# A gather-bound recommendation kernel: another plan of its last 20 steps, and seven more tiles of rows fetched by SyncE and ScalarE

## The chip, the cores and the metric

The kernel runs on one core of a Trainium2 chip. The metric is device time in microseconds (us), the median of several runs; lower is better.

## What is computed

For each of 16,384 samples the kernel looks up 69 item rows and one label row (96 floats each) in a table of 100,001 rows. Every item row gets an attention weight from a small network over the row and the label; the weighted rows are summed in ten groups (windows of 20, 20, 10, 10, 2, 2, 2, 1, 1, 1 rows), and a "top net" of three layers turns the ten sums and the label into one number. Cut to what matters:

```python
u  = emb[batch_user]                       # 16384 x 69 x 96
q  = emb[batch_label[:, 0]]                # broadcast over the 69 rows
z  = concat([q, u, q - u, q * u])
h  = dice(z @ W1 + b1, a1)                 # 64 wide; dice(x) = (a(1-p) + p) x, p = sigmoid(x)
att = (h @ W2 + b2) @ W3 + b3              # one weight per row
pre = where(batch_user < ITEM_NUM, u * att, 0)
pooled = einsum('gf,bfe->bge', window, pre)
x  = concat([pooled, q])
h  = dice(bn(x @ Wf1 + bf1), af1)          # 200 wide
h  = dice(bn(h @ Wf2 + bf2), af2)          # 80 wide
out = h @ Wf3 + bf3
```

## The kernel before

**Tiles and steps.** The samples come in 32 blocks of 512 (`NBLK`, `BLK`). A block's 64 x 512 main rows and 5 x 512 tail rows are 69 chunks (`NCH`) of 512 rows; a chunk is four tiles of 128 rows. Two chunks are a pair, and one step of the plan handles one pair: 1,104 steps (`NPAIR`). A main chunk holds all 64 main rows of eight samples; a tail chunk holds one tail row of all 512 samples. In the last block the tail chunks stand after the first 20 main chunks (`EARLY`, `chunk_of`). `c` is step 1,096, eight before the end; the steps below are named from it (c-12, c+7), and `d` is what follows the last step.

**Fetching.** Most tiles come by an indirect gather of 128 rows that POOL issues (`gather`, line 266). One tile in some chunks (`SLOT`, the fourth) comes row by row instead: SyncE or ScalarE loads the row offsets into registers, 32 at a time (line 286), and issues 128 small DMAs (line 301) into one of 12 ring buffers, 8 for SyncE, 4 for ScalarE (`Singles`). `SP_CHUNKS` lists SyncE's chunks, 199, one every 5.5 steps, each issued six steps ahead; `ACT_CHUNKS` lists ScalarE's, 170. `scalar_rows(i)` issues 20 of ScalarE's rows in step i, so that its DMAs stand in its queue between the activations; 170 x 128 rows at 20 a step last 1,088 steps, up to c-8.

**A step's work**, as functions that record instructions in program order:

- `fetch_of(i)`: the pair's gathers; eight transposes on PE (`ptr`, line 325), for which PE waits for the rows; four DVE operations (`uT`, the product `quT` with the label; lines 376 and 379). `upool` holds 15 pairs.
- `hidden_of(i)`: the 64-wide layer, eight matmul instructions on PE as the profile counts them (`ph`, lines 399 and 403), two activations on ACT and a product on DVE (`y`, lines 405 to 407). It needs the DVE results of `fetch_of(i)`.
- `rows_of(b, n)`: the attention weights of a band of n pairs: a product with a vector `v2` for each pair (`prow`, line 414) and a copy on ACT (`row`, line 416).
- `spread_of(b, n)`: turns a band's weights by four transposes (`patt`, line 431), and DVE lays them out over the windows (`rw`, line 436).
- `pool_of(i)`: the sums of a pair, 16 matmul instructions with the rows as weights (`acc`, line 325), copied to `pooled` by DVE (line 470). There is one PSUM bank for `acc`. It frees the pair's buffer.
- `tails_of(i)`: the weights of tail chunks (`pa`, `pre`; lines 423 and 424).
- the top net (`top_steps`: eight parts of the first layer, four for each half of its width, then `top2`, `top3`; `dice` on ACT and DVE). Its first-layer sums lie in the one bank of `ps_m`, or for some second halves in `ps_h`. The top net of block 30 runs in steps c-20 to c-16; block 31's is cut into four quarters of 128 samples.

Two engines can't be reordered: each one runs its instructions as the plan records them. The plan is written by hand: `at(step, work...)` appends to a step, and steps are played in order. In the steady part, step i records: the weights of a band of four every fourth step, tails (three behind), the spread of the band one step after its weights, the hidden layer of i-2, ScalarE's rows, the sums of i-7 (`POOL_LAG`), and the fetch of i. From c-8 on the old plan lets the sums and hidden layers catch up by a table of its own (lines 635 to 646): bands of four at c-10, c-6, c-2 are spread a step later, later bands begin at c+2, c+5, c+7; quarters 0 and 1 run at c-7 to c-5 and c-3 to c+1; quarter 2 and quarter 3 run in `d`, behind the last fetch.

Of the kernel before, what the change touches and what calls it, by code (L numbers as in the profile page):

```python
# [18 lines left out]
P = 128  # L19
B, F, E, G = 16384, 69, 96, 10  # L20
# [5 lines left out]
BLK = 512  # L26
NBLK = B // BLK
# [5 lines left out]
NQ = BLK // P  # L33
NT = NCH * 4
NCOL = NT + NQ
NPAIR = NBLK * NCH // 2
# [4 lines left out]
POOL_LAG = 7  # L41
# [3 lines left out]
EARLY = 20  # L45

CLOSE = 8


ROW_BYTES = 4 * E  # L50
SLOT = 3
SP_CHUNKS = [2 * (int(5.5 * s) + 6) + 1 for s in range(199)]
SP_RING = 8
ACT_ROWS = 20
ACT_CHUNKS = [2 * ((s + 1) * P // ACT_ROWS + 2) for s in range(170)]
ACT_RING = 4
SINGLES = SP_CHUNKS + ACT_CHUNKS
NSB = (len(SINGLES) + P - 1) // P
# [4 lines left out]
def chunk_of(c):  # L63

    n, k = divmod(c, NCH)
    if n == NBLK - 1 and k >= EARLY:
        k = NMAIN + k - EARLY if k < EARLY + NTAIL else k - NTAIL
    return n, k
# [47 lines left out]
def rec_kernel(  # L116
# [133 lines left out]
    ps_h = ctx.enter_context(tc.tile_pool(name="ps_h", bufs=2, space=PSUM))  # L250
    ps_x = ctx.enter_context(tc.tile_pool(name="ps_x", bufs=2, space=PSUM))
    ps_acc = ctx.enter_context(tc.tile_pool(name="ps_acc", bufs=1, space=PSUM))
    ps_m = ctx.enter_context(tc.tile_pool(name="ps_m", bufs=1, space=PSUM))
# [226 lines left out]
    def dice(x, g, p, b, weights):  # L480

        sb, sa, sna = weights
        nc.scalar.activation(g, p, AF.Sigmoid, bias=sb, scale=S_BN * S_DICE)
        nc.scalar.activation(g, g, AF.Identity, bias=sa, scale=sna)  # L484
        nc.vector.scalar_tensor_tensor(x, p, b, g, ALU.add, ALU.mult)  # L485
# [3 lines left out]
    def top1(n, cols, h, part, p1):  # L489

        if part == 0:

            banks, tag = (ps_h, "h") if n == NBLK - 1 and cols.start >= BLK // 2 and h == 1 else (ps_m, "m")
            p1 = banks.tile([DH, BLK], F32, tag=tag, name=f"p1_{n}_{h}_{cols.start}")[:, cols]
        for k in range(part * KTOP // 4, (part + 1) * KTOP // 4):
            if k < NTAIL:
                w, x = V[:, k], pres[n][:, k, cols]
            elif k == NTAIL:
                w, x = wf1[:, G], qTs[n % 2][0:E, cols]
            else:  # L500
                w, x = wf1[:, k - NTAIL - 1], pooled[n][:, k - NTAIL - 1, cols]
            nc.tensor.matmul(p1, w[:, h * DH : (h + 1) * DH], x, start=(k == 0), stop=(k == KTOP - 1))  # L502
        if part < 3:
            return p1
        g1 = xpool.tile([DH, BLK], F32, tag="g1", name=f"g1_{n}_{h}_{cols.start}")[:, cols]
        dice(x1s[n][:, h, cols], g1, p1, bf1c[h], dice1[h])

    def top2(n, cols):
        x2 = xpool.tile([D2, BLK], F32, tag="x2", name=f"x2_{n}_{cols.start}")[:, cols]
        g2 = xpool.tile([DH, BLK], F32, tag="g1", name=f"g2_{n}_{cols.start}")[0:D2, cols]  # L510
        p2 = ps_m.tile([D2, BLK], F32, tag="m", name=f"p2_{n}_{cols.start}")[:, cols]
        for i in range(2):
            nc.tensor.matmul(p2, wf2[:, i, :], x1s[n][:, i, cols], start=(i == 0), stop=(i == 1))
        dice(x2, g2, p2, bf2c, dice2)
        return x2
# [8 lines left out]
    def store(n):  # L524

        p4 = ps_x.tile([n, P], F32, tag="x", name="p4")
        nc.tensor.transpose(p4, res[:, 0:n], ident)
        r = ypool.tile([P, 512], F32, tag="y", name="r")[0:n, 0:P]
        nc.vector.tensor_copy(r, p4)
        nc.sync.dma_start(out=out[0 : n * P].rearrange("(m p) o -> m (p o)", p=P), in_=r)  # L530
# [9 lines left out]
    pooled, pres, x1s, x2s, qs, us, hs, ys, bands, rws, p1s = ({} for _ in range(11))  # L540

    def top_steps(n, cols):


        def half(h, part):
            if n not in x1s:
                x1s[n] = xpool.tile([DH, 2, BLK], F32, tag="x1", name=f"x1_{n}")
            p1s[n] = top1(n, cols, h, part, p1s.get(n))

        steps = [lambda h=h, part=part: half(h, part) for h in range(2) for part in range(4)]  # L550
        steps.append(lambda: x2s.__setitem__(n, top2(n, cols)))
        if n * BLK + cols.stop < B:
            steps.append(lambda: top3(n, cols, x2s.pop(n)))
        else:
            steps.append(lambda: top3_last(x2s.pop(n)))
        return steps

    def rows_of(b, n):
        return lambda: attend_rows(b, n)

    def spread_of(b, n):
        return lambda: spread(b, n)

    def pool_of(k):
        return lambda: pool(k)

    def hidden_of(k):
        return lambda: ys.__setitem__(k, hidden(k, *hs[k]))

    def tails_of(k):  # L570
        def work():
            uT = hs.pop(k)[0]
            for j in range(2):
                if chunk_of(2 * k + j)[1] >= NMAIN:
                    attend_tail(k, j, ys[k], uT)

        return work

    def fetch_of(k, between=()):
        def work():  # L580
            for j in range(2):
                n = chunk_of(2 * k + j)[0]
                if n not in pooled:
                    pooled[n] = bpool.tile([E, G, BLK], F32, tag="pooled", name=f"pooled{n}")
                    pres[n] = xpool.tile([E, NTAIL, BLK], F32, tag="pre", name=f"pre{n}")
            u, uT, quT = fetch(k, lambda: [w() for w in between])
            us[k], hs[k] = u, (uT, quT)

        return work
# [4 lines left out]
    def at(step, *work):  # L594
        plan.setdefault(step, []).extend(work)

    by_sync = Singles("sp", nc.sync, mybir.EngineType.SP, SP_CHUNKS, 0, range(SP_RING), 32)
    for s, m in enumerate(SP_CHUNKS):
        at(max(0, m // 2 - 6), lambda s=s: by_sync.fetch(s, 0, P))
# [4 lines left out]
        mybir.EngineType.Activation,  # L604
        ACT_CHUNKS,
        len(SP_CHUNKS),
        range(SP_RING, SP_RING + ACT_RING),
        32,
    )
    def scalar_rows(i):  # L610

        row, stop = i * ACT_ROWS, min((i + 1) * ACT_ROWS, len(ACT_CHUNKS) * P)
        while row < stop:
            s, start = divmod(row, P)
            n = min(P - start, stop - row)
            by_scalar.fetch(s, start, start + n)
            row += n

    c = NPAIR - CLOSE
    for i in range(c):  # L620
        if i >= 3 and (i - 3) % 4 == 3:
            at(i, rows_of(i - 6, 4))
        if i >= 3:
            at(i, tails_of(i - 3))
        if i >= 4 and (i - 4) % 4 == 3:
            at(i, spread_of(i - 7, 4))
        if i >= 2:
            at(i, hidden_of(i - 2))
        at(i, lambda i=i: scalar_rows(i))
        if i < c - CLOSE:  # L630
            if i >= POOL_LAG:
                at(i, pool_of(i - POOL_LAG))
        else:

            for k in {0: (-15, -14), 1: (-13,), 3: (-12, -11), 4: (-10, -9), 7: (-8, -7)}.get(i - c + 8, ()):
                at(i, pool_of(c + k))
        at(i, fetch_of(i))

    at(c, pool_of(c - 6), pool_of(c - 5), tails_of(c - 3), hidden_of(c - 2), fetch_of(c))
    at(c + 1, tails_of(c - 2), hidden_of(c - 1), fetch_of(c + 1))  # L640
    at(c + 2, rows_of(c - 4, 4), tails_of(c - 1), hidden_of(c), spread_of(c - 4, 4), pool_of(c - 4), fetch_of(c + 2))
    at(c + 3, pool_of(c - 3), pool_of(c - 2), hidden_of(c + 1), fetch_of(c + 3, [hidden_of(c + 2)]))
    at(c + 4, pool_of(c - 1), fetch_of(c + 4, [hidden_of(c + 3)]))
    at(c + 5, rows_of(c, 4), spread_of(c, 4), pool_of(c), fetch_of(c + 5, [hidden_of(c + 4)]))
    at(c + 6, pool_of(c + 1), pool_of(c + 2), fetch_of(c + 6, [hidden_of(c + 5)]))
    at(c + 7, pool_of(c + 3), rows_of(c + 4, 2), fetch_of(c + 7, [spread_of(c + 4, 2), hidden_of(c + 6)]))

    for n in range(NBLK):
        first, end = n * NCH // 2, ((n + 1) * NCH - 1) // 2
# [12 lines left out]
    for f in range(NTAIL):  # L662
        at(2 + 2 * f, lambda f=f: tail_weights(f))

    quarter = [top_steps(NBLK - 1, slice(r * P, (r + 1) * P)) for r in range(NQ)]
    for s, step in enumerate([1, 1, 1, 2, 2, 2, 2, 3, 3, 3]):
        at(c - 8 + step, quarter[0][s])
    for s, step in enumerate([5, 5, 5, 5, 6, 6, 6, 6, 7, 9]):
        at(c - 8 + step, quarter[1][s])

    d = NPAIR
    at(d, pool_of(c + 4), hidden_of(c + 7), pool_of(c + 5), *quarter[2][0:4], rows_of(c + 6, 2), quarter[2][4])
    at(d, spread_of(c + 6, 2), *quarter[2][5:8], pool_of(c + 6), quarter[2][8], pool_of(c + 7))
    at(d, quarter[2][9], quarter[3][0], lambda: store(B // P - 1), *quarter[3][1:])

    with tc.manual_schedule():
        qs[0] = head_gather(0)
# [76 lines left out]
```

## Time and profile before

| what | us |
|---|---|
| time, median of 9 runs | 10780.31 (10775.26 to 10786.4) |
| the profiled execution's own time | 10801.49 |
| its span, first to last instruction | 10799.7 |
| PE busy (matmuls) | 8768.3 (81%) |
| POOL busy | 8132.1 (75%) |
| DVE busy | 4240.3 (39%) |
| ACT busy (activations alone) | 1883.9 (17%) |

How to read it: times of one engine's instructions; issuing DMAs on SyncE and ScalarE is not counted as busy, and POOL's gathers are counted with 946 ns each, while one starts every 1,252 ns. PE's share is of an engine whose clock is granted in parts: 0.750 of full speed in the mean over the span. The profile puts each idle stretch of an engine down to what ended it ("<-"); "issue" stands for time in which the engine waited for nothing that the profile shows. The profile's lines show an engine, an operation, "out<-in" by the program's names, and "xcount".

### The profile page before, as it was taken

The numbers are of one execution on the slowest core, as the hardware profiler recorded it, in microseconds if no ns is written. First come the engines' busy times: TensorE is split into PE (matmuls) and PEld (weight loads), VectorE is DVE, ScalarE is ACT, GpSimd is POOL, SyncE is SP. The second block draws the span as 40 slices with busy tenths as digits, with TensorE's granted clock in tenths as the row PEclk, the third lists the DMA queues.
The fourth block names the chain that finished last, engine by engine and source line by source line (L and its number), as shares of the span: only waits on it lengthen the run. The fifth ranks groups of instructions, "written<-read, shape, count | busy, mean of one in ns | idle before, by whom it ended". The sixth has DMA issues, their size and how long they took to land.

```text
span 10799.7 us, 204439 instructions
## 1 busy us (share of the span) xinstructions
PE 8768.3 (81%) x41797; PEld 4312.7 (40%) x41797; DVE 4240.3 (39%) x7535; ACT 1883.9 (17%) x2761; POOL 8132.1 (75%) x8597
## 2 busy tenths in 40 slices
PE   6877888878887888877888788888888787887888
PEld 3334434333443343433343334343444343443335
DVE  4333333333333333333333333333343333333333
ACT  1111111111111111111111111111111111111112
POOL 7777777777777777777777777777777777777776
PEclk6777777777777777777777777777777777777778
DMA  2111111212111111111111111111121111111111
GB/s 50 42 42 42 44 42 42 42 42 44 42 42 42 44 42 42 42 42 45 42 42 42 42 44 42 42 42 42 44 42 42 42 42 44 42 42 42 42 42 35
DMA packets 372495, 460.70 MB, mean 43 GB/s; under 512 B 232114, under 2 KB 232626, under 8 KB 371106
## 3 DMA queue, kind: packets, MB, share of 16 engines
q0 software_dynamic: 274912, 422.81, 16.5%
q1 hardware_dynamic: 52802, 16.36, 1.0%
q10 hardware_dynamic: 43520, 8.44, 0.7%
q14 instruction: 925, 7.58, 0.2%
q8 instruction: 336, 5.51, 0.2%
HBM read 446.81 MB, written 0.07 MB: 41 GB/s over the span
## 4 chain that ended last, share of the span: by engine, by line
POOL 39%; PE 21%; issue 18%; DMA 13%; ACTq 6%; ACT 2%; DVE 1%; another core or an unknown queue 0%; POOLq 0%
POOL u L266 39%; DMA u<-in_rows,ids 13%; ACTq L301 5%; PE acc L325 4%; PE p L502 4%; PE ph L399 3%; PE ph L403 3%; PE ptr L325 3%; ACTq L286 1%; PE prow L414 1%; ACT y L405 1%; POOL q L266 1%; PE ph L396 1%; PE pa L423 1%; PE ph L401 0%
## 5 line engine op out<-in xcount | busy, mean ns | idle before, releaser
L266 POOL DMA_INDIRECT u<-in_rows,ids x8463 | 8009.9, 946 | 2585.1 <-issue 2365.9
L325 PE MATMUL ptr<-ident,u 128*96 128x128 f32 x8463 | 1931.1, 332 | 1623.2 <-DMA u<-in_rows,ids 1572.6
L407 DVE TENSOR_TENSOR y<-ph,y 128x512 f32<-128x512 f32 x1104 | 763.5, 692 | 4950.7 <-ACT y L406 4703.3
L325 PEld LDWEIGHTS acc<-rw,u 128*96 128x96 f32 x15702 | 1678.6, 189 | 1333.2 <-issue 855.9
L325 PEld LDWEIGHTS ptr<-ident,u 128*96 128x96 f32 x8463 | 1132.6, 151 | 2303.3 <-DMA u<-in_rows,ids 1867.6
L325 PE MATMUL acc<-rw,u 128*96 128x20 f32 x15702 | 1796.2, 259 | 201.3 <-DVE rw L436 173.4
L376 DVE COPY uT<-ptr 96x512 f32<-96x512 f32 x2208 | 1489.2, 674 | 770.8 <-PE ptr L325 768.4
L405 ACT ACTIVATE y<-ph 128x512 f32<-128x512 f32 x1104 | 658.9, 597 | 6146.9 <-PE ph L403 3452.2
L399 PE MATMUL ph<-uT,A 128*64 128x512 f32 x4096 | 1599.3, 856 | 0.0
L403 PE MATMUL ph<-quT,wn 96*64 96x512 f32 x4416 | 1549.4, 772 | 0.0
L379 DVE TENSOR_TENSOR quT<-ptr,qT 96x512 f32<-96x512 f32 x2048 | 1379.3, 673 | 0.0
L406 ACT ACTIVATE y<-y,wn,na1c 128x512 f32<-128x512 f32 x1104 | 897.9, 813 | 37.2
L403 PEld LDWEIGHTS ph<-quT,wn 96*64 96x64 f32 x4416 | 429.4, 183 | 1004.0 <-issue 1003.3
L502 PE MATMUL p<-pooled,wf 96*100 96x512 f32 (+1 forms) x1400 | 646.3, 607 | 0.0
L414 PE MATMUL prow<-y,v 128*32 128x512 f32 x2208 | 514.5, 878 | 70.2 <-DVE y L407 64.4
L399 PEld LDWEIGHTS ph<-uT,A 128*64 128x64 f32 x4096 | 259.5, 172 | 608.6 <-issue 604.0
L416 ACT COPY row<-prow 128x512 f32<-128x512 f32 (+1 forms) x277 | 161.8, 584 | 1733.2 <-issue 549.9
L470 DVE COPY pooled<-acc 96x160 f32<-96x160 f32 x1008 | 420.5, 417 | 110.4 <-PE acc L325 107.9
L502 PE MATMUL p<-pre,V 96*100 96x512 f32 (+1 forms) x700 | 394.0, 708 | 9.6 <-DVE x L485 9.2
L502 PEld LDWEIGHTS p<-pooled,wf 96*100 96x100 f32 x1400 | 243.5, 186 | 303.9 <-issue 303.9
L436 DVE SCALAR_TENSOR_TENSOR rw<-patt,bb,wn 128x320 f32<-128x320 f32 x554 | 276.0, 538 | 124.6 <-PE patt L431 123.8
L485 DVE SCALAR_TENSOR_TENSOR x<-p,wf,g 100x512 f32<-100x512 f32 (+3 forms) x105 | 73.9, 704 | 516.5 <-ACT g L484 516.5
(72 smaller groups left out, 2716.9 us busy)
## 6 DMA issues: line engine op xcount, KB each, us to landing
ring<-in_rows SPq DMA_DIRECT2D x25472, 0.4 KB
ring<-in_rows ACTq DMA_DIRECT2D x21760, 0.4 KB
u<-in_rows,ids POOLq DMA_INDIRECT x8463
ids<-in_idx SPq DMA_DIRECT2D x8, 560.0 KB, 3.9
q<-in_emb,ids POOLq DMA_INDIRECT x128
wf<-in_far SPq DMA_DIRECT2D x1, 1209.0 KB, 8.8
wn<-in_near SPq DMA_DIRECT2D x1, 236.0 KB, 3.1
offsets<-in_single_rows SPq DMA_DIRECT2D x1, 192.0 KB, 2.5
```

Of the source, the lines that this page charges most:

```text
L266: nc.gpsimd.indirect_dma_start(out=dst, out_offset=None, in_=table, in_offset=bass.IndirectOffsetOnAxis(ap=index, axis=0),)
L301: d = self.engine.dma_start(out=ring[r : r + 1, b], in_=row_bytes[:, bass.ds(self.values[r], ROW_BYTES)]).then_inc(self.sems[k], 16)
L325: ins = op(out, ring[:, at[0]].bitcast(F32) if at else u[:, 4 * (c % 2) + t, :], other, **how)
L376: nc.vector.tensor_copy(uT[j][0:E], ptr)
L379: nc.vector.tensor_tensor(quT[:, j, :].rearrange("e (s f) -> e s f", f=FM), ptr.rearrange("e (s f) -> e s f", f=FM), by_field(q[:, k * NS ...
L399: nc.tensor.matmul(p, As[n % 2][:, k // 4, :], uT[j], start=True, stop=False)
L403: nc.tensor.matmul(p, Wp, quT[:, j, :], start=False, stop=True)
L405: nc.scalar.activation(y, ph, AF.Sigmoid, scale=S_DICE)
L406: nc.scalar.activation(y, y, AF.Identity, bias=a1c, scale=na1c)
L407: nc.vector.tensor_mul(y, ph, y)
L414: nc.tensor.matmul(pr[32 * k : 32 * (k + 1), :], v2, ys[b + k], start=True, stop=True)
L502: nc.tensor.matmul(p1, w[:, h * DH : (h + 1) * DH], x, start=(k == 0), stop=(k == KTOP - 1))
```

## The change

- SyncE's tiles: one every 5.33 steps, 205 instead of 199. ScalarE's tiles: 171 instead of 170, and `scalar_rows` is recorded up to the last steps, so its 128 more rows are issued in steps c-8 to c-2.
- The plan from step c-12 on is written anew. Hidden layers run one step behind their fetch. In odd steps from c-9 on (counted from c) a band of two pairs, i-3 and i-2, is weighted and spread in one step, around the hidden layer of i-1; in even steps the sums of i-4 and i-3 are made. The steps c-12 to c-7 lead over from the old lag of seven.
- The quarters of block 31's top net stand in a table, `QUARTERS`: quarter 0 in c-12 to c-7, quarter 1 in c-5 to c, quarter 2 in c+3 to c+7 with its last part in `d`; quarter 3 remains in `d`, with the first parts of both its halves ahead of the last band.
- Only quarter 3's second half has its sums in `ps_h`; the sums in progress are kept for each half, since the two halves of quarter 3 now overlap.

```diff
+QUARTERS = [
+    [-12, -12, -11, -11, -10, -10, -9, -9, -8, -7],
+    [-5, -5, -5, -4, -3, -3, -3, -2, -1, 0],
+    [3, 3, 3, 4, 5, 5, 5, 6, 7],
+]
-SP_CHUNKS = [2 * (int(5.5 * s) + 6) + 1 for s in range(199)]
+SP_CHUNKS = [2 * (int(5.33 * s) + 6) + 1 for s in range(205)]
-ACT_CHUNKS = [2 * ((s + 1) * P // ACT_ROWS + 2) for s in range(170)]
+ACT_CHUNKS = [2 * ((s + 1) * P // ACT_ROWS + 2) for s in range(171)]
...
-            banks, tag = (ps_h, "h") if n == NBLK - 1 and cols.start >= BLK // 2 and h == 1 else (ps_m, "m")
+            banks, tag = (ps_h, "h") if n == NBLK - 1 and cols.start == BLK - P and h == 1 else (ps_m, "m")
...
-            p1s[n] = top1(n, cols, h, part, p1s.get(n))
+            p1s[n, h] = top1(n, cols, h, part, p1s.get((n, h)))
...
     c = NPAIR - CLOSE
-    for i in range(c):
+    for i in range(c - 12):
...
-        if i < c - CLOSE:
-            if i >= POOL_LAG:
-                at(i, pool_of(i - POOL_LAG))
-        else:
-
-            for k in {0: (-15, -14), 1: (-13,), 3: (-12, -11), 4: (-10, -9), 7: (-8, -7)}.get(i - c + 8, ()):
-                at(i, pool_of(c + k))
+        if i >= POOL_LAG:
+            at(i, pool_of(i - POOL_LAG))
         at(i, fetch_of(i))
 
-    at(c, pool_of(c - 6), pool_of(c - 5), tails_of(c - 3), hidden_of(c - 2), fetch_of(c))
...
-    at(c + 7, pool_of(c + 3), rows_of(c + 4, 2), fetch_of(c + 7, [spread_of(c + 4, 2), hidden_of(c + 6)]))
+    quarter = [top_steps(NBLK - 1, slice(r * P, (r + 1) * P)) for r in range(NQ)]
+
+    for i in range(c - 12, NPAIR):
+        band = i - 3 if (i - c) % 2 and i > c - 11 else None
+        if i == c - 12:
+            at(i, pool_of(c - 19), tails_of(c - 15), hidden_of(c - 14))
+        elif i == c - 11:
+            at(i, pool_of(c - 18), tails_of(c - 14), rows_of(c - 16, 4))
+        elif i == c - 10:
+            at(i, pool_of(c - 17), pool_of(c - 16), pool_of(c - 15))
+        elif i == c - 9:
+            at(i, pool_of(c - 14))
+        elif i == c - 8:
+            at(i, pool_of(c - 13), pool_of(c - 12))
+        elif i == c - 7:
+            at(i, pool_of(c - 11))
+        elif band is None:
+            at(i, pool_of(i - 4), pool_of(i - 3))
+        if band is not None:
+            at(i, rows_of(band, 2))
+        if i > c - 12:
+            at(i, tails_of(i - 2))
+        at(i, hidden_of(i - 1), lambda i=i: scalar_rows(i))
+        if i == c - 11:
+            at(i, spread_of(c - 16, 4))
+        if band is not None:
+            at(i, spread_of(band, 2))
+        for r, steps in enumerate(QUARTERS):
+            at(i, *[work for step, work in zip(steps, quarter[r]) if c + step == i])
+        at(i, fetch_of(i))
...
-    d = NPAIR
-    at(d, pool_of(c + 4), hidden_of(c + 7), pool_of(c + 5), *quarter[2][0:4], rows_of(c + 6, 2), quarter[2][4])
-    at(d, spread_of(c + 6, 2), *quarter[2][5:8], pool_of(c + 6), quarter[2][8], pool_of(c + 7))
-    at(d, quarter[2][9], quarter[3][0], lambda: store(B // P - 1), *quarter[3][1:])
+    d, last = NPAIR, quarter[3]
+    at(d, pool_of(c + 4), hidden_of(c + 7), pool_of(c + 5), quarter[2][9], last[0], rows_of(c + 6, 2))
+    at(d, last[4], lambda: store(B // P - 1), spread_of(c + 6, 2), pool_of(c + 6), pool_of(c + 7))
+    at(d, *last[1:4], *last[5:])
```

More of the change, by code (lines that the diff above doesn't have):

```diff
@@ L629, in rec_kernel @@
         at(i, lambda i=i: scalar_rows(i))
-        if i < c - CLOSE:
-            if i >= POOL_LAG:
-                at(i, pool_of(i - POOL_LAG))
-        else:
-            for k in {0: (-15, -14), 1: (-13,), 3: (-12, -11), 4: (-10, -9), 7: (-8, -7)}.get(i - c + 8, ()):
-                at(i, pool_of(c + k))
-        at(i, fetch_of(i))
-    at(c, pool_of(c - 6), pool_of(c - 5), tails_of(c - 3), hidden_of(c - 2), fetch_of(c))
-    at(c + 1, tails_of(c - 2), hidden_of(c - 1), fetch_of(c + 1))
-    at(c + 2, rows_of(c - 4, 4), tails_of(c - 1), hidden_of(c), spread_of(c - 4, 4), pool_of(c - 4), fetch_of(c + 2))
@@ L642, in rec_kernel @@
[L642 to L645, printed above, removed]
-    at(c + 7, pool_of(c + 3), rows_of(c + 4, 2), fetch_of(c + 7, [spread_of(c + 4, 2), hidden_of(c + 6)]))
+        if i >= POOL_LAG:
+            at(i, pool_of(i - POOL_LAG))
@@ L663, in rec_kernel @@
         at(2 + 2 * f, lambda f=f: tail_weights(f))
[L665 to L669, printed above, removed]
-    d = NPAIR
-    at(d, pool_of(c + 4), hidden_of(c + 7), pool_of(c + 5), *quarter[2][0:4], rows_of(c + 6, 2), quarter[2][4])
-    at(d, spread_of(c + 6, 2), *quarter[2][5:8], pool_of(c + 6), quarter[2][8], pool_of(c + 7))
-    at(d, quarter[2][9], quarter[3][0], lambda: store(B // P - 1), *quarter[3][1:])
+    d, last = NPAIR, quarter[3]
+    at(d, pool_of(c + 4), hidden_of(c + 7), pool_of(c + 5), quarter[2][9], last[0], rows_of(c + 6, 2))
+    at(d, last[4], lambda: store(B // P - 1), spread_of(c + 6, 2), pool_of(c + 6), pool_of(c + 7))
+    at(d, *last[1:4], *last[5:])
     with tc.manual_schedule():
```

## The prediction

> **What bounds the kernel now.** I read the page's table of groups first, then who waited for whom on POOL, then the chain of waits, then the last 300 us as a table by stage, and last the timeline there. On the page and among POOL's waits:
>
> ```profile
> POOL 39%; PE 21%; issue 18%; DMA 13%; ACTq 6%; ACT 2%; DVE 1%; another core or an unknown queue 0%; POOLq 0%
> L266 POOL DMA_INDIRECT u<-in_rows,ids x8463 | 8009.9, 946 | 2585.1 <-issue 2365.9
> POOL u L266 <- issue: 2365.9, 7745, 0.3
> ```
>
> POOL never waits longer than 0.3 us before a gather: 8,591 gathers (128 of them for the labels) run back to back from 3.2 to 10758.6 us, one each 1.252 us, or 9.74 us for one of the 1,104 steps. Up to the last stretch each gather costs its full 1.252 us. The end looks different:
>
> ```profile
> 10498.57 0.45 PE L325 MATMUL ptr<-ident,u 128*96 128x128 f32 x1 [0.85 <-DMA u<-in_rows,ids]
> ...
> 10757.67 0.96 POOL L266 DMA_INDIRECT u<-in_rows,ids  x1 [0.30 <-issue]
> ...
> 10765.26 0.64 PE L325 MATMUL ptr<-ident,u 128*96 128x128 f32 x4
> ...
> 10797.47 0.24 SPq L538 DMA_DIRECT2D out<-r  x1
> ```
>
> The first line is the last time that PE waits for a gather, at step c-20 (c is step 1096). From there the chain of waits holds PE and short ACT and DVE links only. PE's waits from 10498 us to the end, and the stages:
>
> ```profile
> PE acc L325 <- DVE pooled L470: 9.8, 8, 2.7
> PE p L521 <- DVE x L485: 9.2, 2, 7.8
> PE prow L414 <- DVE y L407: 4.7, 2, 4.0
> ...
> PE ptr L325 <- DMA u<-in_rows,ids: 0.8, 1, 0.8
> ```
>
> ```profile
> 10400.00:10498.00 98.00, 76.61 (x330) 35.49 (x329) 41.84 (x73) 15.18 (x22) 74.19 (x79) 0.71 0.17 41
> 10498.00:10591.00 93.00, 82.41 (x369) 39.49 (x370) 32.74 (x57) 15.43 (x22) 70.37 (x75) 0.85 0.17 41
> 10591.00:10766.00 175.00, 146.11 (x847) 91.64 (x847) 75.88 (x139) 37.47 (x59) 126.80 (x134) 0.80 0.16 39
> 10766.00:10800.00 34.00, 28.20 (x220) 23.40 (x218) 7.54 (x19) 7.96 (x17) 0.00 (x0) 0.89 0.01 3
> ```
>
> The first figure after each length is PE's busy time, the 0.71 to 0.89 the granted clock. So 10,500 us are POOL's, and the last 300 us are PE's own: its work, plus 28.9 us of waits from 10591 to 10766 and 5.8 us behind. PE runs some 20 us late at step c-13 and 5 us late at the last step (the last gather starts at 10757.67, its rows reach PE at 10765.26). ACT matters for one reason:
>
> ```profile
> 10594.86 8.64 ACTq L301 DMA_DIRECT2D ring<-in_rows  x20
> 10603.55 0.60 ACT L405 ACTIVATE y<-ph 128x512 f32<-128x512 f32 x1 [7.94 <-issue]
> 10605.77 1.92 PE L414 MATMUL prow<-y,v 128*32 128x512 f32 x2 [4.03 <-DVE y L407]
> ```
>
> ACT issues 20 rows a step in 5.99 us, 8.6 to 8.9 us where a load of 32 addresses falls between them; an activation behind them waits, and here PE with it.
>
> **The change, part by part.** *Gathers.* 376 tiles by row replace 369: seven gathers fewer, 8.8 us by POOL's pace. By step c-20 six are gone (201 SyncE tiles are due by then against 195), so PE leaves its last gather wait 6 x 1.252 = 7.5 us sooner. What comes after is PE's, so I count 7.5; 8.8 is the other end.
>
> *Can SyncE deliver?* The timeline has 503 of its rows in 199.68 us, 0.397 us each, 50.8 us a tile. Tiles are due every 5.33 steps, 51.9 us by the steps' 9.73 us. The first tile's rows are out at 55.7 us and due when step 6 ends, at 78 us; rounding to whole steps eats at most one step of 9.7 us. The lead of some 20 us thus stays positive and grows. I count nothing; if it failed, PE would wait for rows, and POOL's 15 buffers would still let it run on. The 171st ScalarE tile is dearer: rows are issued 20 a step, so 128 more occupy ACT for 6.4 more steps, c-8 to c-2, where it was free before.
>
> *Work moved.* The sums come 3 to 4 steps behind instead of 7, hidden layers one step behind, the last block's quarters earlier. All of it stays inside the stretch that PE bounds, so moved matmuls cost what they cost before: zero. What is seen as a shorter end is paid ahead of it: behind the last transposes stood 31.8 us up to the last store's issue (10765.9 to 10797.5); without quarter 2 (3.56 and 3.84 us of matmuls, and its waits) it is about 23.9, but those 7.9 us are now in steps c+3 to c+7.
>
> *Work added.* Ten bands of two and one of four replace five of four and two of two: four more bands, each one product with v (1.00 us at full clock for two y as for four, 1.74 at half) and four transposes (0.44, 0.80): 5.8 to 10.2 us. I take 5.8, since a slower matmul leaves less of the waits beside it.
>
> *Waits.* In an odd step the new order is: product of the two newest y, hidden layer, transposes of that band, all in one step, where a whole fetch lay between band and transposes before. I lay two steps out from the end of a hidden layer, by the rows (full / half clock): fetch 1.01 / 1.87, hidden 1.90 / 3.61, sum 1.30 / 2.69; y 1.45 on ACT and 0.69 on DVE; copies 2.7 for a pair on DVE. While ACT issues rows, it is free 0.7 + 7.6 us after the hidden layer (7.6 = 5.99 + 0.62 x 2.6), then copies the band in 0.6: PE's transposes start at 8.9, the next sum after y and weights at 11.8, the second sum after DVE's copies at 14.9, the next hidden layer ends at 18.1 (full) or 21.2 (half). PE's work in it is 10.0 or 19.0. At the granted 0.80 (six tenths full) that is 5.7 us of waits in two steps, 4 where parts of the top net fill some. Without rows on ACT the same layout gives 14.6 and 19.9, so 3.1, or 2 with parts. Four pairs of steps of the first kind (c-10 to c-2): 19; four of the second: 10. Beside them the end, with nearly the same last chain of 4 us: 5.8. Together 35, against 28.9 + 5.8 = 34.7: zero. Ends: if ACT's rows cost no wait, its four pairs have 3.1 us in place of 5.7, -10; with a load in every step (8.7 instead of 7.6 us, 2 us a pair) and one dice waiting 7.8 as above, +16. Queued behind PE's wait are the next fetch's transposes, then DVE's copies; POOL does not wait, 15 buffers against a lag of 3 to 4 steps.
>
> The Trainium skill, TensorE: Matmul & The Clock Gate, section "A second HAM failure mode: psum-queue depth-cycling", speaks against the change: a PE that idles briefly between groups of matmuls lets its clock gate swing back to half rate, and bands of two make more such groups. The trace agrees in direction only: 0.71 where PE waits for gathers, 0.85 in the backlog, though single waits there are short. By that rule I would take the steady 0.75 in place of 0.80: 146 x (0.80 / 0.75 - 1) = +10 us in the sum. I leave it out.
>
> *Sum.* -7.5 + 0 + 5.8 + 0 = -1.7 us. The profiled execution took 10801.5 us (span 10799.7, 1.8 around it); -1.7 gives 10799.8. It stands 21.2 us over the median of 10780.3, a difference I leave alone: 10778.6, rounded to 10778.
>
> **Rivals.** *PE catches up.* If PE's waits shrink far enough that it stands beside the last gather again (0.6 us late, as at c-20, not 5), the whole 8.8 us count, and the shorter end too: the last rows land some 1.2 us after the gather's end, 10758.6 + 1.2 - 8.8 = 10751.0, + 0.6 + 0.6 for the transposes, + 23.9, + 2.2 for the store = 10778.3 against 10799.7: -21.4, 10759. For it: PE's work in two steps is 10.0 us at full clock against 19.5 of gathers, which is enough to make up 20 us. Against it: ACT's rows until c-2, and quarters in between. No plan of the end can gain much more.
>
> *ACT's queue decides (slower).* Place: the transposes of bands in c-11, c-9, c-7, c-5, c-3. If PE reaches each while ACT has just begun its rows, each waits a whole issue, 5 x 8.6 = 43 in place of the 19 counted, and one dice behind rows holds the only bank of the top net's sums for 7.8: -1.7 + 24 + 7.8 = +30, 10810. It decides once those waits are over some 43 us together. For it: the 4.03 us above. Against: products and hidden layer lie ahead of the transposes and cover 4 to 6 us.
>
> *The rows come late.* SyncE delivers slower than 51.9 us a tile and PE, not POOL, is held by it: the gain of 7.5 is lost, 10786. Against: 0.397 us a row over hundreds of rows.
>
> **How the numbers follow.** Forecast 0.71, PE catches up 0.16, ACT's queue 0.11, late rows 0.02. 0.2% is 21.6 us, about what a measurement of this kernel can tell from no change. Faster by more: half of the catching up and the forecast's edge, 0.10. Slower by more: ACT's queue and an edge, 0.12. Within: 0.78. The forecast's own range is -12 to +19 by the ends of the waits and bands, 10768 to 10799; from 10758 (PE caught up) to 10799 about 2 in 10 are left out, most of them above.
>
> **What would show it.** POOL: 8,584 gathers in all, the last ending near 10750, still no wait over 0.3 us. PE: last wait for a gather near 10491, last transposes near 10770, not 10765, the end some 24 us behind its last four transposes. Waits of PE from c-12 on: 30 to 40 us, with the transposes of bands (L436 in the new file) waiting for the copy of ACT among the largest; before they had 0.7 us. A clock below 0.78 from c-12 on, or PE waiting for gathers in the last five steps, would prove the sum wrong; so would a POOL wait.

## The result and the profile after

The changed kernel takes 10813.59 us (median of 10 runs, 10809.96 to 10817.09) where the kernel before takes 10780.86 (30 runs): 1.0030 of it [1.0022, 1.0038], or 32.7 us more. Beside each other on another chip, later, the two took 10815.03 and 10782.28: again 32.8. The forecast was 10778, its range ended at 10799.

The two profiled executions stand closer, 10816.73 and 10801.49, because the one of before had slower gathers. From the first gather to the last, one took 1.2520 us there and 1.2494 after; over 8,590 gathers that is 22 us, about the 21 us by which the profile of before stood over its median. So stages are compared from step c-20 on, not from the span's start.

The page of after (the chain of waits by engine; the costliest group) and POOL's waits (total, times, longest):

```profile
POOL 41%; PE 20%; issue 18%; DMA 13%; ACTq 5%; ACT 1%; DVE 1%; another core or an unknown queue 0%; POOLq 0%; DVEq 0%
L271 POOL DMA_INDIRECT u<-in_rows,ids x8456 | 7982.6, 944 | 2581.5 <-issue 2358.9
POOL u L271 <- issue: 2358.9, 7727, 0.3
```

POOL is as before: 8,584 gathers, no wait over 0.3 us. (Line numbers are five higher: 325 is now 330, 399 is 404, 416 is 421.) The end, from the timeline of after:

```profile
10469.42 0.45 PE L330 MATMUL ptr<-ident,u 128*96 128x128 f32 x1 [0.82 <-DMA u<-in_rows,ids]
...
10726.43 0.95 POOL L271 DMA_INDIRECT u<-in_rows,ids  x1 [0.30 <-issue]
...
10780.84 1.04 PE L330 MATMUL ptr<-ident,u 128*96 128x128 f32 x8
...
10812.70 0.24 SPq L543 DMA_DIRECT2D out<-r  x1
```

PE's last wait for a gather is at c-20, as before. But the last transposes stand 54 us behind the start of the last gather, where before 7.6 us lay between them. PE falls further and further back up to step c (61 us, in a table below) and makes up little of it. The windows of after, cut at the end of the last transposes of c-20, c-13, c-10, c and c+7 (length, then busy time with instructions of PE, PE's weight loads, DVE, ACT and POOL, then the granted clock):

```profile
10469.90:10563.00 93.10, 84.24 (x340) 39.83 (x339) 31.20 (x55) 16.83 (x24) 70.19 (x76) 0.78 0.18 42
10563.00:10597.00 34.00, 27.42 (x163) 17.91 (x162) 13.90 (x26) 6.88 (x11) 25.77 (x28) 0.85 0.17 41
10597.00:10720.00 123.00, 93.30 (x486) 59.18 (x484) 39.84 (x78) 20.76 (x35) 93.00 (x99) 0.72 0.17 41
10720.00:10782.00 62.00, 56.65 (x310) 32.97 (x308) 26.45 (x51) 14.22 (x24) 5.67 (x6) 0.81 0.03 6
10782.00:10815.00 33.00, 25.23 (x153) 18.88 (x153) 8.09 (x21) 4.89 (x10) 0.00 (x0) 0.75 0.01 3
```

The same cut made in other kernels' traces; in each field length / PE's idle time / granted clock. 205/170 stands for 205 tiles by SyncE and 170 by ScalarE. The last three columns are kernels of the experiments below; "new plan 205/168" is new_plan_205_168_d.

| stage | before | after | old plan 205/170 | new plan 205/170 | new plan 205/168 |
|---|---|---|---|---|---|
| c-20 to c-13 | 87.8 / 10.0 / 0.85 | 93.2 / 8.9 / 0.78 | 87.8 / 10.2 / 0.85 | 88.1 / 10.4 / 0.85 | 81.7 / 4.6 / 0.88 |
| c-13 to c-10 | 26.2 / 6.8 / 0.80 | 34.1 / 6.6 / 0.85 | 26.2 / 6.2 / 0.74 | 34.6 / 6.1 / 0.85 | 26.5 / 0.6 / 0.87 |
| c-10 to c | 93.7 / 15.2 / 0.80 | 123.1 / 29.7 / 0.72 | 93.7 / 15.2 / 0.80 | 99.0 / 13.7 / 0.79 | 91.5 / 9.6 / 0.81 |
| c to c+7 | 59.1 / 7.0 / 0.80 | 61.7 / 5.2 / 0.81 | 59.0 / 7.0 / 0.80 | 60.0 / 5.3 / 0.86 | 63.8 / 7.5 / 0.86 |
| behind c+7 | 33.8 / 5.5 / 0.89 | 33.1 / 7.8 / 0.75 | 33.8 / 5.5 / 0.89 | 31.6 / 7.8 / 0.80 | 32.8 / 7.1 / 0.71 |
| sum | 300.7 / 44.5 | 345.1 / 58.2 | 300.5 / 44.1 | 313.3 / 43.3 | 296.3 / 29.4 |

After against before: 44.4 us more from c-20 on, while six gathers fewer, 7.5 us by count, lie ahead of it. Of the 44.4 us, 13.7 are idle time; in the other 30.7 PE is busy, with nearly the same work (1,445 matmul records against 1,430), at a mean clock of 0.77 against 0.82. The largest piece is c-10 to c, 29 us. What PE waits for from c-20 on, in after:

```profile
PE ph L404 <- DVE uT L381: 16.9, 3, 8.3
PE acc L330 <- DVE pooled L475: 13.2, 10, 3.4
PE patt L436 <- ACT row L421: 8.8, 3, 4.0
PE p L526 <- DVE x L490: 8.0, 1, 8.0
```

The first line is new: before, from c-20 on, no matmul of a hidden layer waited for `uT`. One of the three, with all that ACT, DVE and PE did around it (start, duration):

```profile
10669.63 8.88 ACTq L306 DMA_DIRECT2D ring<-in_rows  x20
10678.61 0.37 ACT L488 ACTIVATE g<-p,dice 100x128 f32<-100x128 f32 x1 [8.23 <-issue]
10679.01 0.49 ACT L489 ACTIVATE g<-g,dice,dice 100x128 f32<-100x128 f32 x1
10679.42 0.56 ACT L421 COPY row<-prow 64x512 f32<-64x512 f32 x1
...
10679.54 0.35 DVE L490 SCALAR_TENSOR_TENSOR x<-p,wf,g 100x128 f32<-100x128 f32 x1 [8.44 <-ACT g L489]
10679.81 0.68 DVE L381 COPY uT<-ptr 96x512 f32<-96x512 f32 x1
...
10666.95 1.08 PE L404 MATMUL ph<-uT,A 128*64 128x512 f32 x4
...
10669.78 1.04 PE L330 MATMUL ptr<-ident,u 128*96 128x128 f32 x8
10670.75 1.46 PE L419 MATMUL prow<-y,v 128*32 128x512 f32 x4
10680.54 2.31 PE L404 MATMUL ph<-uT,A 128*64 128x512 f32 x3 [8.33 <-DVE uT L381]
```

Read it from top to bottom. ACT issues the step's 20 rows for 8.88 us. The dice activation recorded behind them waits for all of it, though the top net's matmuls that it reads had ended at 10669.94, 0.3 us after the rows began. DVE's half of the dice stands at the head of DVE's own queue and waits with it (8.44 us). Behind it in that queue stand the copies of rows that PE transposed at 10669.78. The next hidden layer needs them, so PE stands for 8.33 us. After that three matmuls take 2.31 us where four took 1.08 us ahead of the wait. A part of it is a wait for the pair's second `uT` copy (10681.00), but the clock has fallen too, from 0.92 ahead of the wait to 0.50 behind it:

```profile
10660.00:10670.00 10.00, 8.82 (x71) 7.31 (x70) 3.24 (x6) 1.03 (x2) 7.56 (x8) 0.92 0.17 40
10680.50:10685.40 4.90, 4.86 (x9) 1.33 (x9) 1.78 (x3) 0.00 (x0) 3.68 (x5) 0.50 0.19 44
```

### The profile page after: what moved, and what is told of

Read it like the earlier page. It is cut to its first block, busy times and chain, and to the rows that moved or that the text cites. A ratio compares the mean times of both kernels' runs of the same rounds, so it can differ in the third digit from the quotient of the medians.

```text
span 10814.9 us, 206305 instructions
## 1 busy us (share of the span) xinstructions
PE 8761.0 (81%) x41813; PEld 4309.5 (40%) x41813; DVE 4243.2 (39%) x7543; ACT 1885.6 (17%) x2765; POOL 8104.5 (75%) x8590
## 4 chain that ended last, share of the span: by engine, by line
POOL 41%; PE 20%; issue 18%; DMA 13%; ACTq 5%; ACT 1%; DVE 1%; another core or an unknown queue 0%; POOLq 0%; DVEq 0%
POOL u L271 40%; DMA u<-in_rows,ids 13%; ACTq L306 4%; PE p L507 4%; PE acc L330 4%; PE ph L404 3%; PE ph L408 3%; PE ptr L330 2%; PE prow L419 1%; ACTq L291 1%; POOL q L271 1%; ACT y L410 1%; PE ph L401 0%; PE pa L428 0%; PE ph L406 0%
## 5 line engine op out<-in xcount | busy, mean ns | idle before, releaser
L404 PE MATMUL ph<-uT,A 128*64 128x512 f32 x4096 | 1602.9, 855 | 17.2 <-DVE uT L381 16.9
L441 DVE SCALAR_TENSOR_TENSOR rw<-patt,bb,wn 128x320 f32<-128x320 f32 (+1 forms) x562 | 277.3, 534 | 111.8 <-PE patt L436 108.3
```

The source lines that it names most:

```text
L404: nc.tensor.matmul(p, As[n % 2][:, k // 4, :], uT[j], start=True, stop=False)
```

## The experiments

**1. The change taken apart.** Two things change: the number of tiles and the plan. Four kernels mix them. Theory Q lays the loss on activations queued behind ScalarE's rows, theory W on the new order of work itself; theories L and F, further down, each lay it on one piece of that order. Each is the kernel before or after with one or two lines of the other:

```diff
 old_plan_205_170 (against before)
-SP_CHUNKS = [2 * (int(5.5 * s) + 6) + 1 for s in range(199)]
+SP_CHUNKS = [2 * (int(5.33 * s) + 6) + 1 for s in range(205)]
 old_plan_205_171: that, and
-ACT_CHUNKS = [2 * ((s + 1) * P // ACT_ROWS + 2) for s in range(170)]
+ACT_CHUNKS = [2 * ((s + 1) * P // ACT_ROWS + 2) for s in range(171)]
 new_plan_199_170: after, with both lists as before
 new_plan_205_170: after, with ACT_CHUNKS as before
```

> The old plan of the end with six more SyncE tiles (205), ScalarE's left at 170. Both theories: six gathers less, all of them ahead of the stretch that PE bounds: 6 x 1.25 = 7.5 us off, 10773 against 10781. If SyncE could not deliver 205 tiles, no gain or a loss, with PE waiting for rows.

> The old plan with 205 and 171 tiles: ScalarE's rows last 6.4 steps longer, to c-2. Theory Q (ScalarE's queue: activations behind rows are late, DVE's operation on them heads DVE's queue, PE waits for the copies behind it): the dice of quarters 0 and 1 now stand behind rows, so it loses: 10785 to 10800. Theory W (it is the new order of work, bands of two and a lower clock, that costs): 8 us off as with 170, 10772.

> The new plan with the old tiles: rows end at c-8. Theory Q: most of the loss goes with the rows of c-8 to c-2, though seven gathers come back: 10795 to 10802. Theory W: the loss stays and the gathers come back: 10820.

> The changed kernel without its 171st ScalarE tile. Theory Q: PE's waits for DVE's copies at c-7 and c-3 (6.3 and 8.3 us) and for bands at c-5 and c-3 go: 15 to 25 us off 10814, 10789 to 10798. Theory W: 10812, unchanged but for one gather.

| kernel (one chip) | us | against before |
|---|---|---|
| before | 10786.68 | |
| old plan, 205/170 | 10777.48 | -9.2, 0.9992 [0.9982, 1.0001] |
| old plan, 205/171 | 10797.87 | +11.2, 1.0010 [1.0001, 1.0020] |
| new plan, 199/170 | 10805.14 | +18.5, 1.0015 [1.0006, 1.0025] |
| new plan, 205/170 | 10793.13 | +6.5, 1.0005 [0.9996, 1.0015] |

Both parts lose. By their distance to before, theory Q put the last three rows at +4 to +19, +14 to +21 and +8 to +17, theory W at -9, +39 and +31: Q holds for two and misses the third by little, W is far off. The six SyncE tiles are worth 9.2 us in the old plan (an interval of -19 to +1, which doesn't exclude zero), 12.0 in the new. The 171st ScalarE tile costs 20.4 us in the old plan, though it saves a gather; in the new plan it costs some 26 (32.7 - 6.5, from two chips). The plan alone, at 205/170, costs 15.6.

The table of stages shows where that lies: from c-20 on PE idles 44.1 us in the old plan and 43.3 in the new, but is busy for 256.4 us in the one and 270.0 in the other, at nearly the same mean clock (0.82 and 0.83). Most of it is the hidden layers, first of old_plan_205_170, then of new_plan_205_170 (number of matmuls, busy time of the line, mean ns of one):

```profile
L403 PE MATMUL ph<-quT,wn 96*64 96x512 f32 x116 | 38.8, 698 | 0.0
L399 PE MATMUL ph<-uT,A 128*64 128x512 f32 x106 | 38.8, 768 | 0.0
```

```profile
L408 PE MATMUL ph<-quT,wn 96*64 96x512 f32 x116 | 48.9, 741 | 0.0
L404 PE MATMUL ph<-uT,A 128*64 128x512 f32 x106 | 47.2, 770 | 2.4 <-DVE uT L381 1.8
```

As many matmuls, of nearly the same mean length, take longer: they lie less over one another. The new plan records a hidden layer one step behind its fetch, ahead of the next fetch, and its weight loads wait 17.2 us for `uT` in 19 short waits, against 1.3 us in 2 in the old plan.

In the old plan the 171st tile costs in another way than in the new one. PE's waits of old_plan_205_171 from c-20 on, and the longest in its timeline:

```profile
PE p L502 <- DVE x L485: 11.2, 1, 11.2
...
PE p L513 <- DVE x L485: 6.0, 2, 4.9
```

```profile
10619.94 8.88 ACTq L301 DMA_DIRECT2D ring<-in_rows  x20
...
10630.05 6.08 ACTq L301 DMA_DIRECT2D ring<-in_rows  x20
10636.17 0.37 ACT L483 ACTIVATE g<-p,dice 100x128 f32<-100x128 f32 x1 [5.38 <-issue]
```

There the parts of a quarter are recorded close together, and the next half of the top net waits for its bank until the dice has read it, 11.2 us. It is the same late activation, with another victim.

**2. The rows behind the dice.** In the changed kernel, `scalar_rows` is recorded behind the parts of the top net:

```diff
-        at(i, hidden_of(i - 1), lambda i=i: scalar_rows(i))
+        at(i, hidden_of(i - 1))
...
-        at(i, fetch_of(i))
+        at(i, lambda i=i: scalar_rows(i), fetch_of(i))
```

> The same kernel as rows_behind_parts, whose first run fell on a chip where SyncE issued a row in 0.666 us instead of 0.397, so that every kernel took 16.7 ms or more and GpSimd and TensorE waited for rows: it says nothing of the last 300 us. Where SyncE delivers, theory Q: 10790 to 10798 beside 10781 of the kernel before (the changed kernel took 10814), TensorE's waits for uT 3 us or less and the clock from c-10 to c 0.78 or more. Rival (the 171st tile costs wherever its rows stand): 10808 to 10818, the waits at the bands or the y instead.

10814.69 us beside 10793.59 of before on its chip: +21.1 us, 1.0018 [1.0009, 1.0027], where the changed kernel stands at +32.8 on another chip. So 11.7 us come back, about half of what was expected. The waits for `uT` are gone from PE's list, and c-10 to c falls from 123.1 to 109.9 us with the clock back at 0.80; but the activations now late are the bands' copies. PE's waits from c-20 on, then two lines of ACT:

```profile
PE patt L436 <- ACT row L421: 19.3, 5, 5.0
PE acc L330 <- DVE pooled L475: 10.6, 10, 1.7
```

```profile
10602.40 8.86 ACTq L306 DMA_DIRECT2D ring<-in_rows  x20
10611.30 0.58 ACT L421 COPY row<-prow 64x512 f32<-64x512 f32 x1 [8.16 <-issue]
```

By the 10780.86 of before that would be 10802, between the two expectations. The queue theory gets about half of what it expected by way of the dice; waits for the next activation took the place of the others, as the rival had said. In both places tried, something that PE needs soon stands behind the 6 to 9 us of row issues.

**3. No rows in the last 20 steps.** ScalarE gets 168 tiles, so that its last rows are issued at c-21; everything else is the new, or the old plan with 205 SyncE tiles.

```diff
-ACT_CHUNKS = [2 * ((s + 1) * P // ACT_ROWS + 2) for s in range(171)]
+ACT_CHUNKS = [2 * ((s + 1) * P // ACT_ROWS + 2) for s in range(168)]
```

> The same kernel as old_plan_205_168, for the same reason. Theory Q (rows behind which activations stand cost, gathers in TensorE's stretch don't): 10770 to 10776 where the kernel before takes 10781 to 10787. Rival (GpSimd's pace still counts to the end): 10778 to 10784.

> The same kernel as new_plan_205_168, for the same reason. Theory Q alone (the plan's loss at 205/170, 15.6 us, is its activations behind rows in c-12 to c-8, but for four more bands): within 8 us above the old plan with 205 and 168 tiles. Theory W (the loss lies in the order of work, which leaves short waits of weight loads and of sums that no longer lie beside other work): 10 to 18 us above it, with the stages c-13 to c-10 and c-10 to c as long as in the new plan with 205 and 170 tiles (34.6 and 99.0 us) or within 3 us of that.

On one chip, before at 10793.59: the old plan takes 10784.16 (-9.4, 0.9990 [0.9981, 0.9999]), the new plan 10780.16 (-13.4, 0.9987 [0.9978, 0.9996]). So without rows the new plan isn't 10 to 18 us behind the old one, as theory W had it, but 4 us ahead (the traces say 2.7: 298.7 against 296.0 us from c-20 on), and the queue theory had expected a small loss for the four bands. The old plan fell short of that theory too: it was to gain some 11 us, and gains no more than with 170 tiles (-9.2). Both plans lose idle time without the rows, the old one 11.7 us, the new one 13.9, and PE remains busy in the new plan for 267 us. What evens them out is the clock of the old plan, 0.67 from c-10 to c where it was 0.80 with 170 tiles:

```profile
10579.20:10688.10 108.90, 93.42 (x489) 63.66 (x487) 40.90 (x75) 20.43 (x34) 82.25 (x87) 0.67 0.20 40
```

What this fall hangs on is not shown; no wait of PE from c-20 on was over 2.6 us there. Two extra gathers cost nothing that shows in the old plan; in the new one PE's last transposes stand beside the last gather (below), so there they may cost. Then the pair that matters, on one chip:

> The new plan with 205 and 168 tiles beside the changed kernel on one chip where SyncE delivers. Theory Q: 40 to 50 us below the changed kernel and 8 to 18 us below the kernel before. Rival (the 46 us came of comparing two chips): less than 35 us below the changed kernel.

> The changed kernel on the same chip: 28 to 38 us above the kernel before; the partner of the new plan with 168 ScalarE tiles.

Before 10782.28, new plan 205/168 10769.27 (-13.0, 0.9988 [0.9979, 0.9997]), the changed kernel 10815.03 (+32.8, 1.0030 [1.0019, 1.0042]): 45.8 us between the last two, for three ScalarE tiles. This is the version that beats both. Its PE waits from c-20 on, and the last transposes:

```profile
PE acc L330 <- DVE pooled L475: 11.0, 9, 1.9
PE ptr L330 <- DMA u<-in_rows,ids: 3.6, 5, 1.1
...
PE ph L404 <- DVE uT L381: 0.5, 1, 0.5
```

```profile
10732.58 0.45 PE L330 MATMUL ptr<-ident,u 128*96 128x128 f32 x1 [0.97 <-DMA u<-in_rows,ids]
```

PE waits for gathers again, up to the very last one. How far PE's last transpose of a step lags behind its landed rows, in us, by the traces:

| kernel | c-20 | c-13 | c-10 | c-4 | c | c+4 | c+7 |
|---|---|---|---|---|---|---|---|
| before | 0.4 | 22 | 19 | 23 | 17 | 8 | 6 |
| old plan 205/168 | 0.4 | 17 | 1.2 | 14 | 12 | 4 | 1.7 |
| new plan 205/170 | 1.1 | 24 | 29 | 32 | 32 | 28 | 22 |
| after | 0.6 | 29 | 33 | 49 | 61 | 57 | 53 |
| new plan 205/168 | 0.4 | 16 | 13 | 8 | 7 | 1.4 | 0.4 |

The old plan bunches the quarters: without rows its PE has caught up by c-10 and then falls back at quarters 0 and 1. The new plan spreads them, which pays only if PE isn't held up meanwhile.

**4. One moved part.** In the old plan with 205/170, quarter 2 goes ahead of the last transposes; in the new plan with 205/168, it goes back behind them. The choice of the bank goes with it both times, and in the new plan the first parts of quarter 3 go back behind the last band, so the two moves aren't quite each other's reverse.

```diff
 old_plan_205_170_q2 (against old_plan_205_170; the ps_h bank as in the change)
-    at(c + 5, rows_of(c, 4), spread_of(c, 4), pool_of(c), fetch_of(c + 5, [hidden_of(c + 4)]))
+    at(c + 5, rows_of(c, 4), spread_of(c, 4), pool_of(c), *quarter[2][0:4], fetch_of(c + 5, [hidden_of(c + 4)]))
...
 (parts 4 to 6 in c + 6, parts 7 and 8 in c + 7, the last in d)
 new_plan_205_168_q2end (against new_plan_205_168)
-    [3, 3, 3, 4, 5, 5, 5, 6, 7],
...
 (d as in the kernel before)
```

> The old plan with 205 and 170 tiles (10777.5 beside 10786.7) and one part of the change: the third quarter of the last block's top net is recorded in steps c+5 to c+7 instead of behind the last transposes. The prediction's reading (moved work costs what it cost before): 0, within 3 us of the old plan with 205 and 170 tiles; the end behind the last transposes falls from 33.8 by 7.9 to about 26 us, and the stage c to c+7 grows by as much. Theory F (the quarter filled waits for y, bands and weights at the end, and fills none where it goes): the end falls by 2 to 4 us only, c to c+7 grows by 6 to 8, and the kernel is 3 to 6 us slower.

> The same kernel as new_plan_205_168_q2end, whose first run fell on a chip that issues SyncE's rows slowly (the kernel before took 16734 us there). Theory F: 4 to 9 us below the new plan with 205 and 168 tiles on the same chip. Rival (TensorE has caught up by c+7, the quarter hides in waits for gathers): 0 to 4 us above it, with a longer end behind the last transposes.

Old plan: 10793.06 beside 10793.59 of before, -0.5, where its partner stands at -9.2: the move costs 8.7 us (by way of before, on two chips, each good to some 10 us; the two traces say 6.8 from c-20 on, 307.3 against 300.5). New plan: 10775.97 with the quarter at the end, 10769.27 with it moved, on one chip, with ranges that don't overlap: the move gains 6.7 us. The windows c to c+7 and behind, first of old_plan_205_170, then of old_plan_205_170_q2:

```profile
10683.60:10742.60 59.00, 52.01 (x286) 30.03 (x285) 29.16 (x53) 12.10 (x18) 38.72 (x41) 0.80 0.18 36
10742.60:10776.40 33.80, 28.32 (x222) 23.53 (x220) 7.54 (x19) 8.09 (x17) 0.00 (x0) 0.89 0.01 3
```

```profile
10692.10:10761.70 69.60, 61.33 (x353) 41.22 (x354) 30.00 (x56) 14.75 (x24) 37.82 (x40) 0.80 0.15 30
10761.70:10791.30 29.60, 22.78 (x152) 17.84 (x151) 6.50 (x16) 5.44 (x11) 0.00 (x0) 0.83 0.01 3
```

The quarter adds 10.6 us where it goes and takes 4.2 from where it was: without it, PE idles 6.8 us at the end instead of 5.5, at a clock of 0.83 instead of 0.89. In the new plan the same two stages are 62.3 and 37.1 us with the quarter at the end, 63.8 and 32.8 with it moved; PE idles 10.4 us in c to c+7 in the first, 7.5 in the second, in part for gathers. There a part of the quarter's work lies in time that PE would have waited anyway. Theory F is right for the old plan, its rival for the new, in direction: both moves were worth more than either had said.

**5. Two chips with a slower SyncE.** Seven runs, among them the first ones of experiments 2 to 4, fell on two chips where the kernel before took 16772.24 and 16734.09 us. All had 205 SyncE tiles, and all were slower than before by 1.0115 to 1.0150, the changed kernel by 1.0150 [1.0133, 1.0167]. Their times tell nothing of the end. SyncE's rows in a stretch of 200 us, in old_plan_205_170, then in old_plan_205_168 and its chain of waits:

```profile
5000.62 199.52 SPq L301 DMA_DIRECT2D ring<-in_rows  x502
```

```profile
5000.57 198.97 SPq L301 DMA_DIRECT2D ring<-in_rows  x299
```

```profile
SPq 63%; issue 36%; PE 1%; another core or an unknown queue 0%; DMA 0%; ACT 0%; DVE 0%; ACTq 0%
```

One row takes 0.397 us to issue on the first chip, 0.665 on the second: there SyncE bounds the whole kernel, and kernels with six more tiles on it are 199 to 246 us slower. Why it is slower there is not known. One kernel ran on such a chip only: the new plan with 205/168 whose hidden layer and bands are recorded inside the next fetch.

> As new_plan_205_168, but the hidden layer of step i-1 and the transposes of a band are recorded within the fetch of step i, behind the transposes of its first chunk, as the old plan did from c+3 on; everything else of the new plan stays. Theory L: the weight loads' waits for uT fall below 4 us in all, and the time lies 8 to 15 us below new_plan_205_168, within 6 us of the old plan with 205 and 168 tiles. Theory W (bands of two, 16 more transposes and the new order of work cost the rest, by the clock or by matmuls that no longer overlap): within 5 us of new_plan_205_168.

Its weight loads waited 3.7 us for `uT` instead of 43.4 in its partner on that chip, but `prow` then waited 16.9 us in 9 times for `y`. Its time, 17009.9 beside 16986.97, is set by SyncE and settles nothing. Its trace does show that the place of the hidden layers makes their matmuls spread out: the lines of `ph` are busy for 44.5 and 41.7 us there, 53.0 and 55.9 in its partner. What that is worth where SyncE delivers was not measured. Theory L's sum fell in another way: in new_plan_205_168_b weight loads still wait 13.6 us for `uT`, in 16 short waits, and the plan isn't behind the old one.

## Why the prediction was wrong

**Where the sum failed.** In its own terms the change is -9.2 for six SyncE tiles, +15.6 for the plan and +26 for the 171st ScalarE tile, against -7.5, +5.8 and nothing of its own. The steps that failed are the waits and the moved work, both put at zero, and with the waits the clock.

**Gathers, -7.5: nothing against it.** Six SyncE tiles gave -9.2 and -12.0, by measurements that tell some 10 us from zero. POOL never waited longer than before, as the rows above show.

**SyncE delivers: right on the chips where a row takes 0.397 us,** and wrong on two others. The rival "the rows come late", given 0.02, is what happens on those.

**The 171st ScalarE tile: wrong.** The prediction wrote that its rows occupy ACT for 6.4 more steps "where it was free before", and gave that no term of its own: within the waits, four pairs of steps with rows stood at 19 us, four without at 10. It measured +20.4 us in the old plan and 26 in the new.

**Waits, zero: wrong, and the main failure, since the 171st tile acts by them.** The layout of two steps placed ACT's rows between the hidden layer and the band's copy, and counted a late dice once, as holder of the one bank of `ps_m`. It did not follow the dice to the next engine: DVE's product at the head of DVE's queue, the copies `uT` behind it, the hidden layer behind those. The question "what is queued behind the waiting instruction" was asked of PE's wait and not of DVE's. Idle time from c-20 on was 58.2 us against 44.5, and in c-10 to c 29.7 against 15.2. The range's upper end took one such dice; there are three (16.9 us), and the bands' copies beside them (8.8).

**Clock at 0.80: wrong.** The prediction had itself named a clock under 0.78 from c-12 on as proof against the sum; c-10 to c had 0.72. PE's busy time there, 93.4 us at 0.72, is 67.2 us of full clock; new_plan_205_170 has 85.3 at 0.79, 67.4: the same work. So of the 24.1 us between these two, 16.0 are idle and 8.1 are clock. From c-13 on the mean was 0.76, against 0.81 before. The rule that was set aside, of the Trainium skill's page TensorE: Matmul & The Clock Gate, section "A second HAM failure mode: psum-queue depth-cycling", pointed the right way. The reason that the prediction took from it, brief idling around bands of two, is not what shows: with the same bands and without the 171st tile, c-10 to c had 0.79. The same page's Part 1 says that the clock halves once PE has idled for a window of some 3.4 us; the clock of 0.50 behind the wait of 8.33 us agrees with it. Long waits aren't the only way to a low clock: the 0.67 of the old plan at 205/168 came with none over 2.6 us.

**Work moved, zero: wrong as a rule.** Quarter 2's move cost 7 to 9 us where PE was late (old plan) and gained 6.7 where PE had caught up. In after, 30.8 us lay between the last transposes and the last store's issue (10781.9 to 10812.7), not 23.9: the matmuls left, but PE idled more behind the last transposes (7.8 against 5.5 us), at a clock of 0.75 against 0.89. And the hidden layers, moved to one step behind their fetch and priced at zero, are the largest part of the 13.6 us for which PE is busy longer in the new plan (experiment 1). That their place just behind the copies is the cause is argued from their weight loads' waits and from one trace on a slow chip; no time shows it.

**Four more bands, +5.8: about right, though no run has them alone.** From the old to the new plan at 205/170 the products with `v` rose from 15.4 to 19.2 us of PE's busy time, the bands' transposes from 5.3 to 7.2: 5.7 us.

**The rivals.** "ACT's queue decides" (10810, chance 0.11) was nearest in time and right in its engine; of its place, the bands in c-11 to c-3, only 8.8 us came true; the dice and the hidden layers did the rest. "PE catches up" (10759, 0.16) did not come with this change. It is what the plan does at 205/168: PE stands beside the last gather, 10769. Its counterargument, "ACT's rows until c-2", was the right one.

## What to carry to other kernels

An engine that issues small DMAs between activations can make an activation that stands ready behind them late by the whole issue; follow that activation through the next engine's queue, not only to its own reader. Moved work is free only in steps where its engine waits for somebody else, so tabulate the lag by step before pricing a move at zero; and work moved close behind what it needs can take longer with as many instructions. Two edits can need each other: the new plan lost 15.6 us with rows up to c-8, 26 more with rows up to c-2, and stood 4 ahead of the old plan once the rows ended ahead of it, where the old plan's clock had fallen.

## What the runs showed that was not expected

- Chips differ in how fast SyncE issues a row: 0.397 us on some, 0.60 to 0.69 (331 rows in 199.50 us, 288 in 199.47) in the traces from two, and with it the kernel before goes from 10.78 to 16.7 ms.
- The gather period is not quite fixed: 1.2520 us in the profile of before, 1.2493 to 1.2509 in the later ones. Over 8,590 gathers that is up to 23 us, more than most edits here are worth. It varies on one chip, too: the profiled execution of new_plan_205_168_b had 1.2493 and stood 12.7 us under its kernel's median, where three other kernels on that chip had 1.2509.
- Behind c+7 the clock was 0.71 in new_plan_205_168_d, whose longest wait of PE from c-20 on was 2.4 us. So a low clock doesn't need a long wait. Whether the short waits lower it, or the small matmuls there, no run separates.
